# A macaron block on one core: first feed-forward with both blocks on each weight group, gate and up weights kept as bfloat16

## The chip, the cores and the metric

The kernel runs on one core of a Trainium2 chip. The metric is the device time of one execution in microseconds (us): the median of the runs. Engines are called PE (TensorE, matrix products; its weight loads appear as PEld), DVE (VectorE), ACT (ScalarE), POOL (GpSimd) and SP (which only issues DMAs here).

## The reference

The input x has 4 batches of 1024 rows of width 512, all float32. Three parts are applied one after the other, each to the normalized rows of the running x:

```
x = x + 0.5 * ffn(layernorm(x))
x = x + attention(layernorm(x))       # 32 query heads, 8 key heads of 16, rope, softmax
x = x + 0.5 * ffn(layernorm(x))       # the same weights again

ffn: w = ternary(w_gate_up), ternary(w_proj)     # per group of 64: sign * scale where |w| is large
     gate, up = split(x @ w_gate_up.T)           # 2 x 2048 columns
     h = silu(gate) * up
     out = rms_norm(h) @ w_proj.T
ternary(w): w to bfloat16; scale = mean(|w|) of 64; q = clip(round(w / scale), -1, 1); (q * scale - w) + w in bfloat16
```

The ternary weights are bfloat16 numbers, so storing them in 16 bits loses nothing.

## The kernel before, in words

Hidden units are cut in 16 groups of 128 (index `hc`), rows in blocks of 512 (index `k` within a stage). For one block and one group, a step of `hidden` (L257) does 16 products of 128x128 by 128x512 into two PSUM banks (`gu`, L267; the normalized input is held as a high part `xT` and a low part `xL`), then `sg` = silu of the gate on ACT (L276), `h = sg * up` on DVE (L278), squares and their sum on POOL (L286, L290), `high`, a rounded copy of h, on ACT (L292), and `low = h - high` on DVE (L294, emitted last in the step as `rest`). `project` (L298) does the 8 products `po` (L306) of an earlier step, one step late in the first stage and two steps late in the others. `end` (L335) scales the sums and adds them to x (L338).

The order of work is: the first feed-forward of batch 0 (label `0a`, 2 blocks), then for each batch attention input and output products, a feed-forward stage and the attention heads. The feed-forward stages after the first work on 2 blocks (32 steps), 4 blocks (64), 4 blocks (64), 2 blocks (32) and 2 blocks (32, the last, with nothing beside it). In the middle ones `early` (L776) puts matrix products `sm` (L724) for the maxima of the coming attention, and DVE reductions `pm` (L733) of them, between the `po` products: 8 a step in the stages of 32 steps, 4 a step in those of 64. Their operands `p_m` come by DMA through `Places.load`. Where code stands in `tc.manual_schedule()` each engine runs its instructions in the order of the program text. The first stage is outside it, so there the instructions are ordered by a scheduler.

In the first stage `prepare` makes the ternary weights of a group (`ternary_weights`) while block 0 uses it: a cast to bfloat16 on ACT (L118), the mean of |w| on DVE (L120), a scale (L124) and its spread over the group on ACT (L126), eight element operations on DVE (L135 to L146), 12 transposes `pw` on PE (L152) and three copies on ACT, two to `guT` (L154) and one to `w_pT` (L156). `guT` (512 KB, float32) is written to `d_guT` in device memory (L157). Block 1 and all later stages read it back with `fetch`, three steps ahead, straight into the tile that the products use (`gate_up`, L98). While block 1 runs, `attention_weights` turns ten tiles of attention weights, each 4 transposes (L172).

## Time and profile before

| | |
|---|---|
| median of 3 runs | 3533.28 us (3523.02 to 3533.41) |
| the profiled execution: own time, span | 3528.59 us, 3526.8 us |
| granted PE clock, mean | 0.983 |

| stage, us from the start of the span | length | PE busy | DVE busy | ACT busy |
|---|---|---|---|---|
| first feed-forward: until the first products | 33 | 5.8 | 25.0 | 11.4 |
| first feed-forward, block 0 (33 to 195) | 162 | 122.6 | 153.0 | 84.1 |
| first feed-forward, block 1 (195 to 297) | 102 | 99.1 | 40.2 | 26.2 |
| second feed-forward stage (355 to 627), 32 steps | 272 | 258.9 | 182.8 | 42.2 |
| third (1045 to 1461), 64 steps | 416 | 409.2 | 251.4 | 86.2 |
| fourth (1877 to 2293), 64 steps | 416 | 409.4 | 251.7 | 85.9 |
| fifth (2706 to 2966), 32 steps | 260 | 256.0 | 182.8 | 43.0 |
| last (3342 to 3527), 32 steps | 185 | 179.2 | 70.3 | 42.6 |

A stage is read by its longest column: where PE is busy nearly all of it, only what PE does or waits for there changes the time. The stretches between these stages are attention and its input and output products.

### The profile page before, as it was taken

The page shows a single profiled execution, that of the slowest core. Times are in us where ns is not written, and L with a number is a line of the kernel's source. Part 1 is how long each engine was busy: PE and PEld are TensorE (multiplying, and loading weights), DVE is VectorE, ACT ScalarE, POOL GpSimd, SP SyncE. Part 2 cuts the span into 40 slices and gives each one's busy share as a digit, 9 for nine tenths or more (in the row PEclk, how much of TensorE's full clock was granted, in tenths as well). Part 3 has the DMA queues.
Part 4 walks back from the last instruction along what each step waited for, and adds up shares of the span by engine and source line. Part 5 has one row for each costly group of instructions (what it writes and reads, how often), then busy time and mean ns, then how long its engine had stood idle before and what let it go on. Part 6 is the DMA issues. An engine that isn't in the chain of part 4 may idle for free.

```text
span 3526.8 us, 55885 instructions
## 1 busy us (share of the span) xinstructions
PE 3377.5 (96%) x22744; PEld 2170.8 (62%) x22744; DVE 2171.9 (62%) x3663; ACT 1499.2 (43%) x1860; POOL 839.5 (24%) x720
## 2 busy tenths in 40 slices
PE   5799899999999999999999999999999999999899
PEld 4577566444487777644467777744457666444587
DVE  8945577677255665577535666577715776774143
ACT  4531111678711222378732222178761113787321
POOL 3353222000043333200023333300013221000144
PEclk9999999999999999999999999999999999999999
DMA  5343333132232342223224333313324232232022
GB/s 179 114 143 120 108 114 101 53 99 89 75 107 97 121 144 98 74 92 99 90 61 123 112 131 104 115 53 106 101 64 116 84 118 90 89 98 71 28 96 90
DMA packets 172192, 349.65 MB, mean 99 GB/s; under 512 B 18080, under 2 KB 84640, under 8 KB 171936
## 3 DMA queue, kind: packets, MB, share of 16 engines
q1 hardware_dynamic: 171936, 346.09, 30.6%
q8 instruction: 179, 2.93, 0.4%
q14 instruction: 77, 0.63, 0.1%
HBM read 283.12 MB, written 62.91 MB: 98 GB/s over the span
## 4 chain that ended last, share of the span: by engine, by line
PE 85%; DVE 7%; DMA 4%; POOL 2%; issue 1%; ACT 1%; SPq 0%; POOLq 0%; DVEq 0%; ACTq 0%
PE gu L267 21%; PE s L821 19%; PE o L842 14%; PE po L306 11%; PE sm L724 8%; PE pa L693 3%; PE gu_0a L267 3%; PE pq L592 2%; DVE pm L733 1%; DMA guT<-d_guT 1%; PE pkv L592 1%; PE po_0a L306 1%; DMA p_m<-d_k 1%; PE pxn L206 1%; DVE x L338 1%
## 5 line engine op out<-in xcount | busy, mean ns | idle before, releaser
L733 DVE TENSOR_REDUCE pm<-sm 128x1 f32<-128x512 f32 x2048 | 1284.8, 683 | 366.2 <-PE sm L724 365.2
L832 ACT ACTIVATE e<-s 128x1024 f32<-128x1024 f32 x1024 | 993.5, 1022 | 284.9 <-PE s L821 280.4
L724 PE MATMUL sm<-p_m,p_m 32*128 32x512 f32 x4096 | 784.7, 442 | 23.1 <-DMA p_m<-d_k 7.6
L267 PE MATMUL gu<-xT,guT 128*128 128x512 f32 x1792 | 711.9, 397 | 7.5 <-DMA guT<-d_guT 7.5
L267 PE MATMUL gu<-xL,guT 128*128 128x512 f32 x1792 | 702.9, 392 | 0.0
L821 PE MATMUL s<-p_s,p_s 32*128 32x512 f32 x4096 | 674.2, 436 | 4.4 <-ACT e L832 4.4
L821 PEld LDWEIGHTS s<-p_s,p_s 32*128 32x128 f32 x4096 | 307.7, 184 | 462.6 <-ACT e L832 445.6
L842 PE MATMUL o<-e,vs 128*32 128x512 f32 x4096 | 549.0, 608 | 1.4 <-ACT e L832 1.4
L724 PEld LDWEIGHTS sm<-p_m,p_m 32*128 32x128 f32 x4096 | 361.1, 184 | 136.8 <-issue 51.9
L276 ACT ACTIVATE sg<-gu 128x512 f32<-128x512 f32 x224 | 133.9, 598 | 694.7 <-PE gu L267 694.7
L286 POOL TENSOR_TENSOR sq<-h 128x512 f32<-128x512 f32 x210 | 218.4, 1040 | 834.2 <-DVE h L278 834.2
L821 PE MATMUL s<-mT,ones_r 2*128 2x512 f32 x2048 | 406.1, 391 | 0.0
L267 PEld LDWEIGHTS gu<-xT,guT 128*128 128x128 f32 x1792 | 339.2, 189 | 92.2 <-DVE pm L733 10.2
L278 DVE TENSOR_TENSOR h<-sg,gu 128x512 f32<-128x512 f32 x224 | 153.8, 686 | 381.1 <-PE gu L267 379.9
L267 PEld LDWEIGHTS gu<-xL,guT 128*128 128x128 f32 x1792 | 339.2, 189 | 69.3
L306 PE MATMUL po<-w_pT,high 128*128 128x512 f32 x896 | 376.5, 420 | 0.0
L306 PE MATMUL po<-w_pT,low 128*128 128x512 f32 x896 | 353.6, 395 | 0.6
L292 ACT CAST high<-h 128x512 fp32r<-128x512 f32 x224 | 139.0, 621 | 463.9 <-DVE h L278 461.1
L675 POOL TENSOR_TENSOR aT<-aT,rec 128x1024 f32<-128x1024 f32 x16 | 37.9, 2370 | 1170.0 <-DMA rec<-d_r 778.8
L290 POOL TENSOR_TENSOR acc<-acc,sq 128x512 f32<-128x512 f32 x205 | 279.3, 1362 | 16.1
L306 PEld LDWEIGHTS po<-w_pT,high 128*128 128x128 f32 x896 | 169.0, 189 | 108.3 <-issue 81.0
L821 PEld LDWEIGHTS s<-mT,ones_r 2*128 2x128 f32 x2048 | 193.0, 184 | 29.3
(129 smaller groups left out, 2890.7 us busy)
## 6 DMA issues: line engine op xcount, KB each, us to landing
guT<-d_guT SPq DMA_DIRECT2D x224, 512.0 KB
p_m<-d_k SPq DMA_DIRECT2D x64, 512.0 KB
p_s<-d_k SPq DMA_DIRECT2D x64, 512.0 KB
p_m<-d_q SPq DMA_DIRECT2D x32, 512.0 KB
p_s<-d_q SPq DMA_DIRECT2D x32, 512.0 KB
d_o<-oT SPq DMA_DIRECT2D x64, 256.0 KB
x<-in_L_attn_x_dram SPq DMA_DIRECT2D x32, 256.0 KB
w<-in_L_ffn_w_gate_up_dram SPq DMA_DIRECT2D x32, 256.0 KB
```

The costliest lines, as they stand in the source:

```text
L267: nc.tensor.matmul(pg, lhsT=self.weights[k, hc][:, c, part, :], rhs=xp[:, c, :], start=(c == 0 and n == 0), stop=(c == DC - 1 and n == 1),)
L276: nc.scalar.activation(sg, gu[0], AF.Silu)
L278: nc.vector.tensor_tensor(h, sg, gu[1], ALU.mult)
L286: nc.gpsimd.tensor_tensor(sq, h, h, ALU.mult)
L290: nc.gpsimd.tensor_tensor(acc, acc, sq, ALU.add)
L292: nc.scalar.copy(high, h)
L306: nc.tensor.matmul(self.pos[k][i], lhsT=h[:, i * P : (i + 1) * P], rhs=w_pT[hc], start=(hc == 0 and n == 0), stop=(hc == HC - 1 and n == 1),)
L724: nc.tensor.matmul(s, lhsT=q[at, i * P : (i + 1) * P], rhs=k[part][at, half * 512 : (half + 1) * 512], start=(part == 0), stop=(part == 1),)
L733: nc.vector.tensor_reduce(pm[:, i, j, half : half + 1], s, AX.X, ALU.max)
L821: nc.tensor.matmul(s[:, e, :], lhsT=k[part][at, keys] if part < 2 else ones_r[at, :], rhs=(q if part < 2 else self.mrows[g])[at, queries], ...
L832: nc.scalar.activation(w, s, AF.Exp, scale=1.0 / HD**0.5)
L842: nc.tensor.matmul(o[j * SLOT : (j + 1) * SLOT, :], lhsT=vs[:, kc, g, :], rhs=es[j // 2][:, j % 2, :], start=(kc == 0), stop=(kc == NT - 1),)
```

## The change

The first feed-forward becomes a class of its own, `First`, with its order written out in `groups`. The 16 groups of weights are prepared over four steps (load and cast; scales; signs; quantize and transpose), and each group is used by block 0 in the step that transposes it and by block 1 two steps later, from the same tile. |2w| is computed on ACT (`double`, Abs with scale 2) instead of by two DVE instructions. Block 1's h of all 16 groups is kept (`h1`); its high and low parts, squares and output products follow after block 0 has ended, with the attention weights among them.

`d_guT` is now bfloat16. The transposed weights are copied to a bfloat16 tile `g16`, written from there, and `widened` makes the float32 tile `guT` that the products use with one ACT copy of 128x1024. Every later stage does the same: `fetch` loads the bfloat16 tile, `widen(n + 1)` stands in the step of n behind `hidden(n)`. There are three buffers of each instead of four of one. The maxima of the second stage start at its step 4 instead of 1 (`begin`), and the operands of the second group of maxima are loaded from a share of 0.05 of a stage on instead of 0. `vs` moves from the constants to `ring`. Only batch 0 of x is loaded at the start; batch 1 follows during the steps.

```
-    d_guT = dram.tile([HC, P, DC * 2 * P], F32, name="d_guT")
+    d_guT = dram.tile([HC, P, DC * 2 * P], BF16, name="d_guT")
     w_pT = [const.tile([P, D], F32R, name=f"w_pT{c}") for c in range(HC)]
-    streamed = ctx.enter_context(tc.tile_pool(name="streamed", bufs=4))
-    vs = const.tile([P, NT, HKV, SLOT], F32, name="vs")
-    nc.gpsimd.memset(vs[:, :, :, HD:], 1.0)
+    streamed = ctx.enter_context(tc.tile_pool(name="streamed", bufs=3))
...
+    def narrow_tile(name):
+        return streamed.tile([P, DC, 2, P], BF16, tag="g16", name=name)
+    def widened(t, name):
+        w = streamed.tile([P, DC, 2, P], F32R, tag="guT", name=name)
+        nc.scalar.copy(w, t)
+        return w
...
-        def __init__(self, blocks, label, prepare=None, beside=None):
-            self.blocks, self.label, self.prepare, self.beside = blocks, label, prepare, beside
-            self.lag = 1 if prepare is not None else 2
+        LAG = 2
+        UNITS = (("h", 2),)
+        def __init__(self, blocks, label, beside=None, begin=0):
+            self.blocks, self.label, self.beside, self.begin = blocks, label, beside, begin
...
         def fetch(self, n):
-            if n < len(self.order) and (self.prepare is None or self.order[n][0] > 0):
+            if n < len(self.order):
                 k, hc = self.order[n]
-                self.weights[k, hc] = gate_up(f"{self.label}_{k}", hc)
+                t = self.narrow[n] = narrow_tile(f"g16_{self.label}_{k}_{hc}")
+                nc.sync.dma_start(t.rearrange("p c g k -> p (c g k)"), d_guT[hc])
+        def widen(self, n):
+            if n < len(self.order):
+                k, hc = self.order[n]
+                self.weights[k, hc] = widened(self.narrow.pop(n), f"guT_{self.label}_{k}_{hc}")
...
+            gate, up = self.products(k, hc)
+            return self.halves(*self.squares(k, hc, self.gated(k, hc, gate), up))
+        def products(self, k, hc):
...
+        def gated(self, k, hc, gate):
+            sg = self.wp.tile([P, 512], F32, tag="sg", name=f"sg_{self.label}_{k}_{hc}", bufs=1)
+            nc.scalar.activation(sg, gate, AF.Silu)
+            return sg
+        def squares(self, k, hc, sg, up):
...
+            nc.vector.tensor_tensor(h, sg, up, ALU.mult)
+            self.tally(k, hc, h)
+            return h, label
...
+        def halves(self, h, label):
...
             nc.scalar.copy(high, h)
...
-                    self.beside(self.ps, (n - 1) / (last - 2), banks)
+                    self.beside(self.ps, (n - self.begin) / (last - 1 - self.begin), banks)
             due = []
-            for n in range(self.AHEAD):
-                if self.order[n] not in self.weights:
-                    self.fetch(n)
             for n, (k, hc) in enumerate(self.order):
                 self.fetch(n + self.AHEAD)
-                if self.prepare is not None:
-                    made = self.prepare(k, hc, self.ps)
-                    if made is not None:
-                        self.weights[k, hc] = made
                 parts, rest = self.hidden(k, hc)
+                self.widen(n + 1)
                 due.append((k, hc, parts))
-                behind = due.pop(0) if len(due) > self.lag else None
+                behind = due.pop(0) if len(due) > self.LAG else None
...
+    class First(FeedForward):
+        UNITS = (("h", 2), ("h1", HC))
+        def run(self):
+            with tc.tile_pool(name="wstage", bufs=1) as stage, tc.tile_pool(
+                name="f0a", bufs=2
+            ) as wp, tc.tile_pool(name="fp0a", bufs=4, space=PSUM) as ps, tc.manual_schedule():
...
+            self.first.__exit__(None, None, None)
+        def tally(self, k, hc, h):
+            if k == 0:
+                super().tally(k, hc, h)
+        def late_tally(self, hc, h):
+            sq = self.wp.tile([P, 512], F32, tag="sq", name=f"sq_0a_1_{hc}", bufs=1)
+            if hc == 0:
+                acc = self.wp.tile([P, 512], F32, tag="acc", name="acc_0a_1")
+                self.accs[1] = [acc]
+                nc.scalar.square(acc, h)
+            else:
+                acc = self.accs[1][0]
+                nc.scalar.square(sq, h)
+                nc.gpsimd.tensor_tensor(acc, acc, sq, ALU.add)
+        def load(self, hc):
+            if hc >= HC:
+                return
+            w = self.stage.tile([P, 12, P], F32, tag="w", name=f"w_{hc}")
...
+        def cast(self, hc):
+            if hc < HC:
+                self.wb[hc] = self.sixteen("wb", hc, 3)
+                nc.scalar.copy(self.wb[hc], self.w.pop(hc).rearrange("p c k -> p (c k)"))
+        def double(self, hc):
+            if hc < HC:
+                self.twice[hc] = self.sixteen("twice", hc, 2)
+                nc.scalar.activation(self.twice[hc], self.wb[hc], AF.Abs, scale=2.0)
+        def scales(self, hc):
+            if hc >= HC:
+                return lambda: None
...
+            mean = small.tile([P, ng], F32, tag="wmean", name=f"wmean_{hc}")
+            nc.vector.tensor_reduce(mean, by_group, AX.X, ALU.add, apply_absolute_value=True)
+            scale = small.tile([P, ng], BF16, tag="wscale", name=f"wscale_{hc}")
+            nc.vector.tensor_scalar(scale, mean, 1.0 / GROUP, 1e-8, ALU.mult, ALU.max)
+            def widen():
+                self.wide[hc] = self.sixteen("wide", hc)
+                nc.scalar.copy(
+                    self.wide[hc].rearrange("p (a k) -> p a k", k=GROUP),
+                    scale.unsqueeze(2).to_broadcast([P, ng, GROUP]),
+                )
+            return widen
+        def signs(self, hc):
+            if hc >= HC:
+                return
+            bits, wide, mask = mybir.dt.uint16, self.wide.pop(hc), self.twice[hc]
+            nc.vector.tensor_tensor(mask, mask, wide, ALU.is_gt)
+            q = self.q[hc] = self.sixteen("wq", hc)
+            nc.vector.tensor_scalar(
+                q.bitcast(bits), self.wb[hc].bitcast(bits), 0x8000, None, ALU.bitwise_and
+            )
+            nc.vector.tensor_tensor(q.bitcast(bits), q.bitcast(bits), wide.bitcast(bits), ALU.bitwise_or)
+        def quantize(self, hc):
+            if hc >= HC:
+                return
+            q, wb, mask = self.q[hc], self.wb.pop(hc), self.twice.pop(hc)
+            nc.vector.tensor_tensor(q, q, wb, ALU.subtract)
+            nc.vector.tensor_tensor(q, q, wb, ALU.add)
+            nc.vector.tensor_tensor(q, q, mask, ALU.mult)
+        def transpose(self, hc):
+            q = self.q.pop(hc)
+            w16 = narrow_tile(f"g16_{hc}")
+            for part in range(3):
+                pt = self.ps.tile([P, DC, P], BF16, tag="gu", name=f"pw_{hc}_{part}")
+                for c in range(DC):
+                    at = (part * DC + c) * P
+                    nc.tensor.transpose(pt[:, c, :], q[:, at : at + P], ident16)
+                if part < 2:
+                    nc.scalar.copy(w16[:, :, part, :], pt)
+                else:
+                    nc.scalar.copy(w_pT[hc].rearrange("p (c k) -> p c k", k=P), pt)
+            nc.sync.dma_start(d_guT[hc], w16.rearrange("p c g k -> p (c g k)"))
+            self.weights[0, hc] = self.weights[1, hc] = widened(w16, f"guT_{hc}")
...
+        def groups(self):
+            for i in range(4):
+                load_x(0, i)
+            self.load(0)
+            for i in range(4, NT):
+                load_x(0, i)
+            for turn in self.normalize(0, [0, 1, 2, 3], self.wp, self.ps, "gu"):
+                turn()
+            self.cast(0)
+            self.load(1)
+            widen = self.scales(0)
+            widen()
+            self.double(0)
+            self.cast(1)
+            self.load(2)
+            widen = self.scales(1)
+            self.signs(0)
+            self.cast(2)
+            self.load(3)
+            self.double(1)
+            widen()
+            self.quantize(0)
+            units, parts, sg, made = {}, {}, {}, {}
+            def finish(k, c):
+                if (k, c) in made:
+                    units[k, c] = self.squares(k, c, sg.pop((k, c)), made.pop((k, c))[1])
+            def start(k, c):
+                made[k, c] = self.products(k, c)
+                sg[k, c] = self.gated(k, c, made[k, c][0])
+            for i in range(HC + 2):
+                finish(0, i - 1)
+                if 2 <= i:
+                    for some in ([0, 1], [2, 3]):
+                        self.project(0, i - 2, parts[0, i - 2][0], some)
+                widen = self.scales(i + 2)
+                if (0, i - 1) in units:
+                    parts[0, i - 1] = self.halves(*units.pop((0, i - 1)))
+                    parts[0, i - 1][1]()
+                if i < HC:
+                    self.transpose(i)
+                self.signs(i + 1)
+                if i < 2:
+                    for turn in self.normalize(1, [2 * i, 2 * i + 1], self.wp, self.ps, "gu"):
+                        turn()
+                if i >= 2:
+                    start(1, i - 2)
+                self.cast(i + 3)
+                self.load(i + 4)
+                self.double(i + 2)
+                widen()
+                if i >= 2:
+                    finish(1, i - 2)
+                if i < HC:
+                    start(0, i)
+                self.quantize(i + 1)
+                if 2 <= i < 2 + NT:
+                    load_x(1, i - 2)
+            self.end(0, self.factors(0))
+            turns = {}
+            for n in range(2):
+                turns[n] = self.attention_weights(n)
+            def split(c):
+                h, label = units.pop((1, c))
+                parts[1, c] = self.halves(h, label)
+                self.late_tally(c, h)
+            for c in range(2):
+                split(c)
+                parts[1, c][1]()
+            for c in range(HC):
+                if c + 2 < HC:
+                    split(c + 2)
+                self.project(1, c, parts[1, c][0], [0, 1])
+                if c in turns:
+                    turns[c]()
+                self.project(1, c, parts[1, c][0], [2, 3])
+                if c + 2 < HC:
+                    parts[1, c + 2][1]()
+                if c + 2 < 10:
+                    turns[c + 2] = self.attention_weights(c + 2)
+            self.end(1, self.factors(1))
...
                         then.fetch(n)
                 for turn in then.normalize(0, [i], wp, ps, "pt"):
                     turn()
+                if i == 3:
+                    then.widen(0)
...
             for at, kind, g in (
-                (0.0, "m", 1),
+                (0.05, "m", 1),
                 (0.3, "m", 2),
...
-    for b in range(2):
-        for i in range(NT):
-            load_x(b, i)
-    with tc.tile_pool(name="wstage", bufs=2) as stage:
-        FeedForward([(0, tb, "a") for tb in range(NB)], "0a", prepare=prepare).run()
+    First([(0, tb, "a") for tb in range(NB)], "0a").run()
     ring = ctx.enter_context(tc.tile_pool(name="ring", bufs=4, side="right"))
+    vs = ring.tile([P, NT, HKV, SLOT], F32, tag="vs", name="vs", bufs=1)
+    nc.gpsimd.memset(vs[:, :, :, HD:], 1.0)
...
-        return FeedForward(blocks, f"{b}", beside=at[b].early if b < B else None)
+        return FeedForward(blocks, f"{b}", beside=at[b].early if b < B else None, begin=4 if b == 0 else 1)
```

## The prediction

> **What bounds the kernel now.** First the page: PE is busy 96% of the span, so a change counts where PE does more, does less, or waits. Then the stretches of the stages (columns: length; busy time and instructions of PE, PEld, DVE, ACT, POOL; granted PE clock; DMA share; GB/s).

> ```profile
> PE 3377.5 (96%) x22744; PEld 2170.8 (62%) x22744; DVE 2171.9 (62%) x3663; ACT 1499.2 (43%) x1860; POOL 839.5 (24%) x720
> ```
> ```profile
> 33.00:195.00 162.00, 122.55 (x572) 91.01 (x571) 153.02 (x182) 84.10 (x111) 66.44 (x30) 0.89 0.36 120
> 195.00:297.00 102.00, 99.14 (x463) 81.68 (x461) 40.20 (x60) 26.21 (x44) 45.89 (x38) 0.98 0.44 142
> 3342.00:3527.00 185.00, 179.22 (x809) 148.12 (x807) 70.32 (x97) 42.60 (x69) 85.22 (x68) 0.99 0.26 91
> ```

> Block 0 of the first stage is DVE's (153 of 162 us), block 1 and the last stage are PE's. So the first stage has something to win: weight preparation on DVE could lie beside the PE work of both blocks. The later stages have nothing but waits to win, and PE must not be made to wait. The timeline of one step of the last stage (start, duration, engine) shows how much room there is between the last gate/up product and the first weight load of the next step:

> ```profile
> 3386.28 0.39 PE L267 MATMUL gu<-xL,guT 128*128 128x512 f32 x1
> 3386.78 0.69 DVE L278 TENSOR_TENSOR h<-sg,gu 128x512 f32<-128x512 f32 x1 [2.44 <-PE gu L267]
> 3387.50 0.62 ACT L292 CAST high<-h 128x512 fp32r<-128x512 f32 x1 [1.96 <-DVE h L278]
> 3388.10 0.19 PEld L267 LDWEIGHTS gu<-xT,guT 128*128 128x128 f32 x1
> ```

> The room is 3388.10 - 3386.28 = 1.82 us, the eight `po` products at 0.227 each. In a 64-step stage four pairs of `sm` products lie there too, and it is 1135.90 - 1133.17 = 2.73:

> ```profile
> 1133.17 0.39 PE L267 MATMUL gu<-xL,guT 128*128 128x512 f32 x1
> ...
> 1134.41 0.62 ACT L292 CAST high<-h 128x512 fp32r<-128x512 f32 x1 [1.98 <-DVE h L278]
> ...
> 1135.90 0.19 PEld L267 LDWEIGHTS gu<-xT,guT 128*128 128x128 f32 x1
> ```

> Waits that PE has now at the start of such stages, from the timelines (idle time in brackets):

> ```profile
> 374.85 0.79 PE L724 MATMUL sm<-p_m,p_m 32*128 32x512 f32 x2 [6.82 <-DMA p_m<-d_q]
> 380.58 0.79 PE L724 MATMUL sm<-p_m,p_m 32*128 32x512 f32 x2 [4.93 <-DMA p_m<-d_k]
> 1074.77 0.77 PE L267 MATMUL gu<-xT,guT 128*128 128x512 f32 x1 [3.86 <-DMA guT<-d_guT]
> ```

> Durations come from the groups of the first 400 us, shapes kept apart (busy us, mean ns):

> ```profile
> L120 DVE TENSOR_REDUCE wmean<-wb 128x24 f32<-128x1536 bf16 x16 | 27.8, 1740 | 0.7 <-ACT wb L118 0.7
> L118 ACT CAST wb<-w 128x1536 bf16<-128x1536 f32 x16 | 23.4, 1472 | 6.8 <-DVE wq L145 6.8
> L292 ACT CAST high_0a<-h_0a 128x512 fp32r<-128x512 f32 x32 | 19.8, 620 | 52.0 <-DVE h_0a L278 52.0
> ```

> **The widening in the later stages.** Before, the product tile came by DMA. Now ACT must copy 128x1024 into it, and `widen(n + 1)` stands behind `hidden(n)`: in ACT's order behind `high(n)`, which waits for `h(n)`, which waits for the last product of step n. ACT has idle time (42.6 of 185 us busy in the last stage), but not at that place. The trace has no widening of this shape. Between the two rows a further element costs (1472 - 620) / 1024 = 0.83 ns, so 1024 elements take 620 + 512 x 0.83 = 1046 ns (bounds: 620 and 1472, by the rows on both sides; I take 1046). Queued instructions on ACT follow at 0.09 us less than their length, so it starts 0.53 after `high`. From the last product's start: 0.50 to h, 0.72 to high, 0.53 to the widening, 1.05 for it, 0.05 to the weight load: 2.85 us. PE waits 2.85 minus the room, in every step. Counting rooms in the stage timelines:
> - last stage: 2 steps without `po` (room 0) 5.7; 24 with 1.82 give 24.7; 4 with 2.37 (transposes) 1.9; one at the block boundary, where h is 1.3 us later, 1.3 more. **+33.6.**
> - each 64-step stage: 2 with room 0 5.7; 8 with 1.82 8.2; 33 with 2.73 4.0; the others have over 3. 17.9. Against that the wait for `guT` ends (3.86 and 3.61 idle, and 16 products at half clock after it, 5.87 us instead of 3.4: 6.2 together): PE is 5.7 later there anyhow, the tile has half the bytes, and the maxima's second load no longer goes ahead of it on SP's queue. `pm` waits of PE (10.2 us in all stages) take in perhaps 1. **+11 each.**
> - second stage: 5.7, and three more steps without maxima at 1.03. Its waits for `p_m` go, since the maxima start at step 4 and PE has work until then: 6.82 + 4.93 idle, and 14 products at half clock, 2.8. **8.8 - 14.5 = -6.** The 208 pairs of maxima still fit, 8 in each of the 26 steps left.
> - fifth stage: rooms of 3.9 and more, so only 5.7, against a `p_m` wait of 2.7 and 1.7 of half clock after it that the 5.7 cover. **+1.**
> - Clock: after the 2.81 us gap of PE that ended at 354.56 the granted clock is 0.50 from 356.2 to 359.6; gaps of 1.1 us and less mostly leave it. So the 2.85 us waits at the start of the five stages cost about one such stretch each, half of 3.4 us. **+8.5** (bounds 0 and 17).

> [...]

> Later stages together: 33.6 + 22 - 6 + 1 + 8.5 = **+59**.

> **The first stage, anew.** The written order makes the head serial. Statistics of four tiles end at 7.4 and `rstd` at 9.0. With one `xn` buffer and program order each tile then takes 0.59 (xn), 1.15 (cold transposes), 0.6 (copy), 0.6 (xL) = 2.95 us: 20.8. Only behind the fourth copy may ACT cast group 0: 21.5. `w` has one buffer, so group 1 is loaded then; a 512 KB load took 3.25 (`p_in`, 293.70), 768 KB I estimate at 5: cast at 28.0. Reduce, scale, `signs(0)`, `quantize(0)` on DVE (1.74, 0.17, 2.2, 2.6, as issued) end at 34.6; group 0's transposes started at 31.7 before. Steps 0 and 1 each hold the normalizing of two tiles in series before their products: about 17 and 18.7 us, so 70.5.

> In the 14 full steps: PE 12 transposes 0.75 (a group of them in block 0), 32 products 7.26, 8 `po` 1.82: 9.8. DVE, at start-to-start distances: reduce and scale 1.76, is_gt and the other four tensor operations 0.87 each, the and 0.47, two h 1.2, low 0.9: 8.7. ACT: three of 1.38, three copies 1.5, widening 0.95, two sg 1.0, high 0.53: 8.1. PE is last, barely; at 10.0 a step: 210.5. The widening here has cover: it is done 4.9 us after the step began and the products on it start at 6.1. Two last steps of 5.45: 221.4.

> Then a wait is added. Block 1's `po` use the banks of block 0's, and `low(1, 0)` stands on DVE behind the four updates of x: 0.9 for the sums, then ms 0.16, power 1.02, half 0.17, hand-overs 0.4, updates 2.73, low 0.98: PE idle 5.5, end 227.8. The 16 output steps (29.1), ten weight tiles (0.55 each, the difference of rooms 2.37 and 1.82) and a cold start 1.7: 264. Final sums and updates 5.5: 269.5; the first attention product, at 297.08 before, follows at about 272. **-25.** SP's new order (single buffers of `w`, stores of 256 KB) hides under 10 us steps; without that cover a load would show its 5.

> Bounds: PE alone needs 16 x 9.8 + 29 + 5.5 + 4 for normalizing = 196 us behind a head of 35 and ahead of 5.5 at the end, and the attention product is 2.5 later: 239, -57. If Abs and Square needed two table loads a step (a load took 1.28; no row shows these functions, so 0 to 2.56), steps would be 10.7 and the output steps 4.2 instead of 2.2: 10 + 32 more, +17.

> **Sum.** 3528.6 + 59 - 25 = 3562.6 of the profiled execution's own time; the median lies 4.7 above that execution. 3567.

> **Rivals.**
> - The first stage wins little: with PE, ACT and DVE within 1.8 us of each other, small waits make a step 11.5 instead of 10; 14 x 1.5 = 21 of the 25 are gone, 3588. For it: every engine waits on two others, and POOL stretches some DVE instructions (`low` 1.75 instead of 0.7 once). Against: each hand-over above has slack of 0.2 to 3 us.
> - The first stage comes near its limit, -57: 3535, no change. For it: PE is last in a step even now. Against: the head and steps 0 and 1 are serial by the text.
> - Faster: the widening is off PE's path. One mechanism: ACT runs it while PE is in the products of step n (ACT idles 2.2 us before `sg`). Then nothing is added later, the waits removed stay removed (6.2 x 2, 14.5, 4.4: 31), and with -25 it is 3477. It decides from a widening that starts 1.03 us earlier than behind `high` in the last stage. Against: in the timeline `low` of step 2 of the second stage starts at 386.97, 17 us after its input, exactly behind the reductions that the text puts before it, so the text's order is kept.
> - The change doesn't do what it says (block 1 still reads its weights): the code gives both blocks one tile; no weight.

> **How the numbers follow.** About 0.3% (10.6 us) can be told from no change: 3522.7 to 3543.9. The likeliest case has 0.62; the first stage winning little 0.18; near its limit 0.10; widening off the path 0.10. So slower 0.80, same 0.10, faster 0.10. The range goes from 3535 (-57 in the first stage with the rest as summed) to 3600 (nothing won, clock at its upper bound): it leaves out the fast rival and, with the tails of the others, no more than 2 in 10.

> **What would show it.** In the profile after: a group of ACT casts `guT<-g16` 128x1024 near 1046 ns, x224, each starting 0.53 behind `high`; PE weight loads waiting for it, near 1 us in most steps of the last stage, whose length goes from 185 to some 220; the second stage without its `p_m` waits; the first attention product near 272. Wrong would be: no PE wait on the widening (fast rival), or steps of the first stage over 11 us.

## The result, and the profile after

The kernel after takes 3572.19 us (median of 4 runs, 3567.13 to 3575.67) against 3532.24 us before (median of 4): the ratio is 1.0118, 95% interval 1.0096 to 1.0139. It is 1.2% slower, 5 us above the forecast. The profiled execution took 3575.67 us (span 3573.9), the longest of the four, and the one of before (3528.59) lies below its own median; so the two spans differ by 47.1 us where the medians differ by 40.

From the page of after, the busy time of PE and the costliest groups around the widening (busy us, mean ns of one, idle time of the engine before them and what ended most of it):

```profile
PE 3395.9 (95%) x22736; PEld 2172.5 (61%) x22736; DVE 2151.9 (60%) x3629; ACT 1755.7 (49%) x2132; POOL 788.1 (22%) x703
L200 PE MATMUL gu<-xT,guT 128*128 128x512 f32 x1792 | 726.3, 405 | 57.3 <-ACT guT L97 56.5
L200 PEld LDWEIGHTS gu<-xT,guT 128*128 128x128 f32 x1792 | 343.1, 191 | 178.5 <-ACT guT L97 93.3
L97 ACT CAST guT<-g 128x1024 fp32r<-128x1024 bf16 x240 | 250.2, 1044 | 1.2 <-PE gu_0a L200 1.2
```

The widening costs 1044 ns, and weight loads wait 93.3 us for it. The stretches of the first stage and of the last stage to the end, after (length; busy time of PE, PEld, DVE, ACT, POOL; granted clock; DMA share; GB/s):

```profile
33.00:221.50 188.50, 166.33 (x856) 135.75 (x856) 154.86 (x187) 133.07 (x166) 38.33 (x33) 0.96 0.30 97
221.50:270.03 48.53, 39.90 (x182) 30.96 (x181) 21.27 (x40) 23.01 (x40) 24.32 (x22) 0.89 0.39 115
3355.40:3573.90 218.50, 190.14 (x810) 147.57 (x808) 70.61 (x97) 71.61 (x100) 85.27 (x68) 0.99 0.14 44
```

The first stage now has PE, DVE and ACT side by side, and the first attention product starts at 270.03 instead of 297.08. The last stage has grown from 185.0 to 218.5, with nearly the same PE instructions in it. One step of it, from the timeline of after:

```profile
3423.00 0.39 PE L200 MATMUL gu<-xL,guT 128*128 128x512 f32 x1
3423.49 0.69 DVE L220 TENSOR_TENSOR h<-sg,gu 128x512 f32<-128x512 f32 x1 [2.90 <-PE gu L200]
3424.21 0.62 ACT L242 CAST high<-h 128x512 fp32r<-128x512 f32 x1 [1.96 <-DVE h L220]
3424.74 1.04 ACT L97 CAST guT<-g 128x1024 fp32r<-128x1024 bf16 x1
3425.83 0.19 PEld L200 LDWEIGHTS gu<-xT,guT 128*128 128x128 f32 x1 [1.06 <-ACT guT L97]
```

The weight load of the next step comes 2.83 us behind the start of the last product, where the eight `po` would have let it come at 1.82. In 30 of the 31 steps the room is 2.8 or 2.9 us.

In the second stage two steps (21 and 29) have rooms of 9.24 us where their neighbours have 5.0. The timeline shows PE waiting for the end of a chain on DVE, its matrix products `sm` queued behind:

```profile
522.29 0.22 DVE L917 TENSOR_REDUCE m<-pm 128x32 f32<-128x64 f32 x1
522.55 1.08 DVE L920 CAST mst<-m 128x32 fp32r<-128x32 f32 x1
523.66 0.21 DVE L921 TENSOR_TENSOR mst<-m,mst 128x32 fp32r<-128x32 f32 x1
524.02 0.39 PE L929 MATMUL pmT<-ident,mst 128*64 128x128 f32 x1 [2.00 <-DVE mst L921]
```

The stages of all kernels, worked out from the timelines of their profiled executions: the start of the second stage's first gate/up product, and for each stage the time from there to the start of its last one (us).

| kernel | second starts | second | third | fourth | fifth | last |
|---|---|---|---|---|---|---|
| before | 355.3 | 269.7 | 414.2 | 414.3 | 257.3 | 171.5 |
| after | 330.9 | 287.5 | 422.2 | 422.4 | 265.1 | 204.9 |
| e1, widening first | 331.3 | 271.3 | 408.0 | 408.1 | 253.8 | 171.8 |
| e2, float32 later | 330.5 | 273.7 | 407.8 | 407.9 | 256.9 | 171.5 |
| e3, turn later | 331.2 | 272.2 | 425.4 | 425.1 | 262.3 | 205.2 |
| e4, head interleaved | 328.0 | 287.5 | 422.1 | 422.2 | 258.9 | 206.3 |
| e5, split widening | 331.1 | 278.0 | 417.0 | 419.2 | 262.6 | 190.6 |
| e6, bfloat16 alone | 364.9 | 268.6 | 422.2 | 422.2 | 265.0 | 205.0 |
| e7, e1 from step 1 | 331.9 | 267.8 | 407.6 | 407.6 | 253.1 | 171.5 |
| e8, e1 + e3 + e4 | 327.8 | 263.0 | 407.6 | 407.7 | 253.4 | 171.5 |
| e9, after again | 331.8 | 284.0 | 422.0 | 422.5 | 260.8 | 208.3 |

So 24.4 us are won up to the second stage, and 17.8 + 8.0 + 8.1 + 7.8 + 33.4 = 75.1 are lost in the later ones; the stretches between them make up the rest (3.6 shorter).

### The profile page after: what moved, and what is told of

Read it like the earlier page. It is cut to its first block, busy times and chain, and to the rows that moved or that the text cites. A ratio compares the mean times of both kernels' runs of the same rounds, so it can differ in the third digit from the quotient of the medians.

```text
span 3573.9 us, 56028 instructions
## 1 busy us (share of the span) xinstructions
PE 3395.9 (95%) x22736; PEld 2172.5 (61%) x22736; DVE 2151.9 (60%) x3629; ACT 1755.7 (49%) x2132; POOL 788.1 (22%) x703
## 4 chain that ended last, share of the span: by engine, by line
PE 85%; DVE 6%; ACT 3%; DMA 2%; POOL 2%; issue 1%; SPq 0%; DVEq 0%; POOLq 0%; ACTq 0%
PE gu L200 22%; PE s L992 18%; PE o L1013 14%; PE po L256 9%; PE sm L895 8%; PE gu_0a L200 3%; PE pa L864 3%; DVE h L220 2%; ACT guT L97 2%; PE pq L763 1%; PE po_0a L256 1%; DVE pm L904 1%; PE pkv L763 1%; ACT high L242 1%; DVE x L288 1%
## 5 line engine op out<-in xcount | busy, mean ns | idle before, releaser
L200 PE MATMUL gu<-xT,guT 128*128 128x512 f32 x1792 | 726.3, 405 | 57.3 <-ACT guT L97 56.5
L200 PE MATMUL gu<-xL,guT 128*128 128x512 f32 x1792 | 710.3, 396 | 0.0
L200 PEld LDWEIGHTS gu<-xT,guT 128*128 128x128 f32 x1792 | 343.1, 191 | 178.5 <-ACT guT L97 93.3
L97 ACT CAST guT<-g 128x1024 fp32r<-128x1024 bf16 x240 | 250.2, 1044 | 1.2 <-PE gu_0a L200 1.2
```

The source lines that it names most:

```text
L97: nc.scalar.copy(w, t)
L200: nc.tensor.matmul(pg, lhsT=self.weights[k, hc][:, c, part, :], rhs=xp[:, c, :], start=(c == 0 and n == 0), stop=(c == DC - 1 and n == 1),)
```

## The experiments

**e1: the widening written ahead.** Two lines of `chunks` change places.

```
+                self.widen(n + 1)
                 parts, rest = self.hidden(k, hc)
-                self.widen(n + 1)
```

> Only the place of the widening changes: widen(n + 1) is written ahead of hidden(n), so that ACT copies the tile before sg(n) and high(n), in the time in which PE is in the products of step n. Theory (what costs is the place in ACT's order, not the copy's 1.04 us nor the bfloat16 fetch): PE's waits for the tile go; the rooms of the last stage return from 2.85 to 1.82 us and the stage from 218.5 to about 185; the 64-step stages lose 13 to 16 us each, the second stage 8 and the fifth 7. Sum -77: about 3495 us (3485 to 3510). Rival A (the bfloat16 tile arrives too late, or ACT has no 1.04 us free in a step, so that the wait moves to sg or high): 3560 us or more. Rival B (half of the waits return as later sg or h): about 3530.

Measured: 3483.51 us (3478.64 to 3489.04), ratio 0.9869 (0.9852 to 0.9887) to before. Of the waits for `guT`, 56.5 us of PE and 93.3 of its weight loads in after, 0.4 and 1.1 are left. The same place in the last stage, timeline of e1:

```profile
3335.09 0.39 PE L200 MATMUL gu<-xL,guT 128*128 128x512 f32 x1
3335.59 0.69 DVE L220 TENSOR_TENSOR h<-sg,gu 128x512 f32<-128x512 f32 x1 [2.39 <-PE gu L200]
3336.31 0.62 ACT L242 CAST high<-h 128x512 fp32r<-128x512 f32 x1 [1.96 <-DVE h L220]
3336.84 1.04 ACT L97 CAST guT<-g 128x1024 fp32r<-128x1024 bf16 x1
3336.91 0.19 PEld L200 LDWEIGHTS gu<-xT,guT 128*128 128x128 f32 x1
```

The copy runs at the same place as in after, 0.53 behind `high`, and is as long. But it makes the tile of the step after the next one, so the weight load at 3336.91 does not wait for it: it starts while the copy runs. The 1.04 us of ACT cost nothing; what cost was that the copy stood in the order one step before its use, behind the end of that very step. The time is 11 us under what was expected and just below its range: the last and the 64-step stages gave what was said, but the second stage gave 16.2 for 8 and the fifth 11.3 for 7, because half clock went there too: after has it for 41 us of the second stage and for 14 of the fifth, e1 for 26 and for none.

**e2: the new first stage with float32 weights.** `d_guT` is float32 and written from the widened tile; `fetch` loads it into `guT` (four buffers); `widen` does nothing, and `g16` has one buffer.

```
-                t = self.narrow[n] = narrow_tile(f"g16_{self.label}_{k}_{hc}")
-                nc.sync.dma_start(t.rearrange("p c g k -> p (c g k)"), d_guT[hc])
+                t = streamed.tile([P, DC, 2, P], F32R, tag="guT", name=...)
+                self.weights[k, hc] = t
+                nc.sync.dma_start(t.rearrange("p c g k -> p (c g k)").bitcast(F32), d_guT[hc])
```

> The first stage keeps the new order of the change, but the gate and up weights lie in memory as float32 (written from the widened tile) and the later stages fetch them straight into the product tile, four buffers, no widening in a step. Theory (the two halves of the change have opposite signs: the new order gains 25, the widening costs the rest): first attention product at 270 us as in the kernel after, within 2; the last stage 185; third and fourth stage 414; the second stage 250 to 270, since the maxima still start at step 4. Time about 3508 us (3493 to 3517), 64 below the kernel after. Rival (the first stage's gain needs the smaller stores and loads of bfloat16): first attention product at 285 or later, 3525 us or more.

Measured: 3493.96 us (3489.38 to 3502.76), ratio 0.9907 (0.9886 to 0.9928). The first attention product starts at 269.64, so the first stage's gain needs no bfloat16. It came out 14 below the middle of what was expected, because the third and fourth stage fell to 408, not 414. So the wait of before for `guT` there goes without any change in its bytes. What is left of the change at that place is that the maxima's second load no longer stands ahead of the fetch; that is argued, and was not tried alone. In e6, which keeps that load where before has it, PE has no wait over 1.5 us for `guT` in those stages from step 3 to step 20 either, with half the bytes and a later PE; so the load order is one way to lose the wait and not the only one. The second stage missed the expected 250 to 270 with 273.7, and it is the one place where the bytes may count. PE's waits in the second stage of e2 (us in total, times, longest):

```profile
PE gu L199 <- DMA guT<-d_guT: 9.2, 1, 9.2
PE pmT L928 <- DVE mst L920: 4.0, 2, 2.0
```

The 9.2 us wait for a 512 KB tile behind the maxima's operands on SP is in no kernel with bfloat16 tiles.

**e3: the turn one step later.** A turn is the transpose `pmT` of a group's maxima with what follows it. `early` remembers its step and takes a turn only in a later one.

```
+            self.now = share
-            if n == 4 and self.turning:
+            if n == 4 and self.turning and self.stamp != share:
                 self.turning.pop(0)()
...
             self.turning.append(turn)
+            self.stamp = getattr(self, "now", None)
```

> The turn of a group's maxima (transpose and what follows) is taken one step later when the group's last maximum was found in the same step of the 32-step stages. Nothing else changes. Theory (in the second stage steps 21 and 29 have rooms of 9.24 us against 5.0, because the transpose waits 2.0 us for the DVE chain pm, m, mst, and the clock halves afterwards): both rooms return to about 5 and the half-clock stretches after them go; second stage from 287.5 to about 274, in all -13: about 3559 us. Rival (the long rooms are queueing of the maxima behind DVE and stay, with the transpose only moved): second stage within 4 us of 287.5, 3570 us.

Measured: 3564.95 us (3562.9 to 3567.9), ratio 1.0100 (1.0085 to 1.0115) to before, 7 below after. The second stage of before, after and e3 (columns as above), and PE's longest waits in it in after (first two lines) and e3:

```profile
355.27:625.02 269.75, 256.69 (x1188) 169.57 (x1188) 181.82 (x310) 41.48 (x69) 72.86 (x65) 0.97 0.33 106
330.89:618.39 287.50, 272.97 (x1184) 177.97 (x1183) 183.93 (x308) 71.77 (x101) 73.93 (x65) 0.93 0.23 72
331.22:603.38 272.16, 261.64 (x1184) 171.00 (x1183) 183.43 (x308) 71.81 (x101) 73.97 (x65) 0.98 0.25 76
```
```profile
PE gu L200 <- ACT guT L97: 8.5, 5, 4.1
PE pmT L929 <- DVE mst L921: 4.0, 2, 2.0
PE gu L200 <- ACT guT L97: 8.2, 5, 3.8
PE sm L895 <- DVE pm L904: 1.6, 3, 0.8
```

The rooms of steps 21 and 29 are 5.96 each, the 2.0 us waits and the half-clock stretches behind them (10.24 us each in after, from 523.71 and 598.80) are gone, and the second stage is 272.2, 15.3 shorter. The median was missed by 6, though the two profiled spans differ by 12.8 (3573.9 and 3561.1), near the 13 that were expected; why the medians differ by less is not shown. In the profile of e3 the third and fourth stage are 3 longer each, with two half-clock stretches at the start of each that after does not have (in the third, products follow at 0.43 us instead of 0.23 from 1026.4 and 1033.2 on), and the fifth is 2.8 shorter. That led to e9.

**e4: the head interleaved.** Cast, scales, doubling and signs of group 0 stand between the four normalized tiles.

```
-            for turn in self.normalize(0, [0, 1, 2, 3], self.wp, self.ps, "gu"):
+            for i, turn in enumerate(self.normalize(0, [0, 1, 2, 3], self.wp, self.ps, "gu")):
                 turn()
+                if i == 0:
+                    self.cast(0)
+                    self.load(1)
+                if i == 1:
+                    self.scales(0)()
...
```

> Only the head of the first stage changes: the cast, scale, doubling and signs of group 0 stand between the four normalized tiles instead of behind them. Theory (the head is serial as written, and what follows starts when group 0's bits are ready): group 0's transposes at about 28.5 us instead of 35.4, all later times of the first stage 7 earlier, first attention product at 263, about 3565 us. Rival (steps 0 and 1 are bound by the weights of groups 1 and 2 or by the normalizing of block 1, so an earlier head only waits there): transposes earlier, but the first attention product at 268 or later, 3570 us.

Measured: group 0's transposes at 32.70 instead of 35.44, the first attention product at 267.18 instead of 270.03; 3572.14 us (3567.55 to 3578.68), no difference from after that the spread lets through. The mechanism held, since all that follows moved by the same 2.7 to 2.9. The size did not, with 7 expected: `xL` of the third tile now waits 4.31 us for its copy `xT`, which stands on ACT behind the spread, the doubling and the cast of group 1 (17.20 to 21.32).

**e5: the widening in two halves**, still behind `hidden(n)`.

```
-        nc.scalar.copy(w, t)
+        for half in range(2):
+            c = slice(half * DC // 2, (half + 1) * DC // 2)
+            nc.scalar.copy(w[:, c], t[:, c])
```

> The widening stays behind hidden(n), but is two copies of 128x512 instead of one of 128x1024, the half that PE needs first copied first. Theory (PE waits for the chain last product, h 0.50, high 0.72, next copy 0.53, its length; a copy of 128x512 takes about 0.62, and PE needs the second half only after 4 products, 0.9 us later): the floor of the rooms falls from 2.85 to about 2.42 us; last stage from 218.5 to 205, third and fourth -6 each, second and fifth -2 each: about 3543 us (3538 to 3555). Rival (the first weight load waits for the whole tile): two copies end about 0.1 later than one, rooms of 2.95, 3575 us.

Measured: 3538.19 us (10 runs, 3526.78 to 3552.98), ratio 1.0029 (1.0010 to 1.0048). In the last stage of e5 (timeline):

```profile
3379.29 0.39 PE L202 MATMUL gu<-xL,guT 128*128 128x512 f32 x1
3381.03 1.14 ACT L99 CAST guT<-g 128x512 fp32r<-128x512 bf16 x2
3381.70 0.19 PEld L202 LDWEIGHTS gu<-xT,guT 128*128 128x128 f32 x1
```

The weight load follows after 3381.70 - 3379.29 = 2.41 us, inside the two copies: it waits for the first half alone. The floor is 2.41 to 2.44 and the last stage 14.3 shorter. The third and fourth stage are 5.2 and 3.2 shorter where 6 was expected, the second 9.5 where it was 2. The chain that the prediction summed is the one that PE waits for.

**e6: bfloat16 alone.** The kernel before, with the weights in memory as bfloat16, `widen(n + 1)` behind `hidden(n)` and a 16-bit tile in `ternary_weights`; first stage in its old order, maxima from step 1.

```
-                self.weights[k, hc] = gate_up(f"{self.label}_{k}", hc)
+                t = self.narrow[n] = narrow_tile(f"g16_{self.label}_{k}_{hc}")
+                nc.sync.dma_start(t.rearrange("p c g k -> p (c g k)"), d_guT[hc])
...
                 parts, rest = self.hidden(k, hc)
+                self.widen(n + 1)
```

> The other half of the change alone, on the kernel before: gate and up weights in memory as bfloat16, widened by ACT behind hidden(n), three buffers of each; the first stage keeps its old order (block 1 reads its weights back, as bfloat16), the maxima start at step 1 as before. Theory (the two halves add up): last stage 218, third and fourth 422, fifth 265, second stage 5 to 9 longer than the 269.7 of before; first attention product at 297 within 8, as its order is left to the scheduler, which now has one more ACT copy to place: 3532 + 65 = about 3597 us (3585 to 3612). Rival (half the bytes of the fetch pay for part of it, or block 1 of the first stage also waits for its widenings, 16 times 1.03): below 3575, or above 3612.

Measured: 3594.89 us (3593.72 to 3600.05), ratio 1.0188 (1.0168 to 1.0209). The total and four stages are as expected. Two parts were not. The second stage is 1.1 shorter than before, not longer: the waits for `p_m` end when their DMAs land, and they swallow the waits for the widening that stand ahead of them. And the first attention product comes at 306.73, 9.7 later than before: there the products wait for the widening too. From PE's waits of e6:

```profile
PE gu_0a L277 <- ACT guT L103: 15.4, 8, 2.2
```

**e7: e1 with the maxima from step 1.** `begin=4 if b == 0 else 1` becomes `begin=1`.

> The kernel with the widening written first (e1_widen_first), but the maxima of the second stage start at step 1, as in the kernel before, not at step 4. Theory (the later start only exchanges costs: the 11.7 us of p_m waits and 2.8 of half clock return, and the two rooms of 9 us with their half clock, 11 to 13 together, go, since the maxima are no longer packed 8 to a step): second stage within 4 of the 271.3 of e1_widen_first, time 3480 to 3488. Rival (the prediction's step: the waits return and nothing goes): second stage about 285, 3497 us.

Measured: 3482.02 us (3475.96 to 3486.65), ratio 0.9865 (0.9842 to 0.9887), the same as e1. PE's waits in the second stage of e7:

```profile
PE sm L895 <- DMA p_m<-d_q: 6.3, 1, 6.3
PE sm L895 <- DMA p_m<-d_k: 4.4, 1, 4.4
```

The waits are back, and the stage is 3.5 shorter than in e1 (267.8 against 271.3). In sums over the 31 rooms and 32 steps: e1 has 2.5 us less between the products, but its products take 118.7 instead of 112.8, slowed by the half clock behind the long rooms (26 us of half clock in e1's stage). Started at step 4, steps carry 8 pairs each, but for one of 6 (step 19). So the second group of 64 ends in the first of the three calls of step 21, and the third in that of step 29, and their turns fall into the second call of the same step. Started at step 1, steps of 6 and 8 alternate, and no room is over 5.8 behind the waits for `p_m`.

**e8: e1, e3 and e4 together.**

> Three edits together on the kernel after: the widening ahead of hidden(n), the turn of the maxima one step later, and the interleaved head. Theory (they touch different stages and waits, so their gains add): 3483.5 less 9.4 (rooms 21 and 29 back to 5.96: 2.6 + 3.3, half clock after them 3.9, less 0.4 of two transposes moved into rooms of 5.2) less 2.8 (head) = about 3471 us. Rival (what the rooms save is given back in other stages by the clock, as e3_turn_later gave back 6 of its 15): 3478 us or more.

Measured: 3471.83 us (3465.8 to 3473.69), ratio 0.9831 (0.9807 to 0.9855): the fastest, 57 us below the runs of before beside it and 100 below after. The second stage is 263.0, shorter than from step 1 on: with the turn moved, the later start pays.

**e9: the kernel after once more.**

> The kernel after, unchanged, profiled once more, to test a rule for the clock read from the profiles so far: every half-clock stretch begins on a grid of 3.413 us that starts anywhere in a run, and of the 2.45 us waits of PE at the start of steps 1 and 2 of the third, fourth, fifth and last stage those that lie with 2.0 us or more in one cell of the grid are followed by half clock in the next cell, those that a grid line cuts into pieces of 1.8 us or less are not. Theory: the eight waits of this run follow that rule, whichever stages it now hits, and a stage with two such stretches is about 3 us longer (third and fourth 422.3 without, 425.3 with two; fifth 262 without either). Rival (the stages differ by themselves, by what stands ahead of their waits): as in the first profile of this kernel, half clock in the fifth stage twice and in the others not at all, wherever the grid lies.

Measured: 3579.98 us, a single execution. Stretches of this run, one per cell of the grid, in the fifth stage (first four) and the last (columns as above; the clock is the third number from the end):

```profile
2719.27:2722.68 3.41, 2.40 (x11) 1.65 (x9) 0.69 (x1) 1.67 (x3) 1.03 (x2) 1.00 0.26 88
2722.68:2726.09 3.41, 1.97 (x9) 1.62 (x10) 0.98 (x1) 1.39 (x2) 0.91 (x1) 1.00 0.46 149
2726.09:2729.51 3.42, 1.96 (x9) 1.30 (x7) 0.69 (x1) 1.18 (x3) 0.59 (x1) 1.00 0.25 85
2729.51:2732.92 3.41, 2.37 (x10) 1.99 (x11) 0.93 (x1) 1.15 (x3) 2.07 (x2) 1.00 0.23 80
...
3360.97:3364.38 3.41, 1.47 (x6) 1.24 (x7) 1.27 (x2) 1.56 (x2) 1.04 (x1) 1.00 0.15 24
3364.38:3367.80 3.42, 3.42 (x9) 2.63 (x8) 0.00 (x0) 0.60 (x1) 0.00 (x0) 0.50 0.14 53
3367.80:3371.21 3.41, 0.96 (x4) 0.48 (x3) 1.72 (x2) 1.56 (x2) 1.75 (x2) 1.00 0.00 0
3371.21:3374.62 3.41, 3.41 (x9) 2.67 (x8) 0.00 (x0) 0.10 (x1) 0.89 (x1) 0.50 0.25 77
```

In the fifth stage the grid cuts both waits (1.00 and 1.45, 1.46 and 1.05 us) and the clock stays. In the last stage pieces of 1.94 and 2.45 us lie in one cell each (PE busy 1.47 and 0.96 of 3.41), and the next cell has half clock. In the first profile of this kernel it was the other way round: half clock twice in the fifth stage (pieces of 2.31 and 2.40), none in the last (1.70 and 1.25 at most). The waits of the third and fourth stage are cut too (1.61 and 1.63 at most) and have none. So seven of the eight waits are as the rule says, the rival falls, and the fifth stage is 260.8 here against 265.1. The eighth, cut into 0.54 and 1.94, lies between the two bounds of the rule (1.8 and 2.0): the cell behind the 1.94 has half clock.

## Why the prediction was right, and where not

**The widening's place.** The chain is right in each term: 1044 ns for 1046, 0.53 behind `high`, 2.83 us for 2.85. That the last stage gives +33.5 for +33.6 is luck in part. Up to the weight load its 31 rooms grew by 33.9 in sum (55.9 to 89.8), but up to the product the time grew by 27.9 only (61.9 to 89.8). The rest, 5.5, is in the products: the second product starts 0.34 behind the first where it was 0.23 in most steps, and one step has half clock (5.14 for 3.54). e1 and e5 show the cause: the same copy one step earlier costs nothing, and half of it takes 0.43 from each room. The fast rival also had its price right: e1 gives 3483.5 where it said 3477.

**The 64-step stages.** +8.0 and +8.1 for +11. The wait for `guT` went as said (e1: 414.2 to 408.0, 6.2 for 6.2), and by e2 it goes without the smaller bytes. The widening costs 422.2 - 408.0 = 14.2, not 17.9: the rooms, up to the weight load, grew by 18.7 in sum, but a product whose weight load has waited starts with it (both at 3425.83 in the last stage of after), where otherwise it starts 0.22 behind it (3422.32 and 3422.54 there). So the time between products grew by 12.0 only, and 2.2 are in the products. That term was measured up to the weight load, one instruction short of the product.

**The second stage.** +17.8 for -6: the mis-sized term. The `p_m` waits of PE did go. What failed is "The 208 pairs of maxima still fit, 8 in each of the 26 steps left", taken at no price. They fit, but packed so that two turns fall into the step of their last maximum. e3 takes that away alone and the stage loses 15.3; of this the two rooms are 2 x 3.3, and the products behind them, half of the time at half clock, 2.3 + 2.4. The remaining 4 lie in other half-clock stretches. That leaves 8 of the 24 by which the term was off. With the widening off PE's path and the turn moved (e8), the stage is 6.7 shorter than before, where the prediction has 14.5 for the ended waits. Of the 7.8 that are missing, 5.6 lie at step 18: its room is 8.35 in e8 and 5.49 before, and the products behind it take 6.1 and 3.4, with the clock at 0.50 from 476.13 to 482.95. In e2, where no half clock falls there, the room is 6.53 and the products take 3.5. e7 shows that without the widening, too, the later start gains nothing until the turn is moved (e8). And e6 shows the 8.8 for the widening to be nothing at all where a DMA wait follows.

**The fifth stage.** +7.8 for +1, and yet the term was right: in e4, whose grid cuts both waits, it is 258.9, +1.6 against before. The rest is clock: two stretches of 3.41 us behind its two waits and a third of 6.83 at 2872 us that e4 does not have either (e9, with the waits cut but that third stretch, has 260.8).

**Clock.** 8.5, one stretch of half clock for each of five stages. It is no fixed sum: behind these waits it fell twice on the second and fifth stage in after and not at all on the third, fourth and last; in e3 twice on the third and fourth; in e9 twice on the last. Two stretches make a stage about 3 longer (422.2 against 425.4).

**The first stage.** -24.4 up to the second stage for -25. Group 0's transposes came at 35.44 (34.6), steps 0 and 1 ended at 71.6 (70.5), the last step at 220.6 for 221.4 after steps of 9.86 (10.0), PE idle 3.49 + 1.72 for 5.5, the first attention product at 270.03 for 272. The two table loads a step that the slow bound allows for did not come: both profiles have 10 in all.

**Sum.** By spans +47.1 for +34.1. The second stage is 23.8 over its term, the fifth 6.8, the first 0.6; the 64-step stages are 5.9 under theirs; the 8.5 for the clock, summed apart, lies in the stages; and the stretches between them are 3.6 shorter. In medians it is +40 for +34, because the profiled run of before lies low among its runs and that of after high. So the mechanism of the widening and that of the first stage were right, but that 3567 came within 5 of 3572 is luck: 31 us of terms too low were met by 18 us too high, and the choice of profiled runs took 7 of the other 13.

## What to carry to other kernels

When a load is replaced by a load and a conversion, the conversion needs a distance ahead of its own: written in the step before its use, behind work that ends with that step, even 1 us on a half-idle engine stands on the critical path, and one line moved earlier takes it off (here 89 us between after and e1). Before delaying work to fill a wait, look at what the tighter packing does to the hand-overs at group ends. Measure a room up to the product and not up to its weight load.
